# A two-layer attention and feed-forward kernel: the first layer's feed-forward and the second layer's attention rounds written as one program

## The chip, the cores and the metric

The kernel runs on one core of a Trainium2 chip. The metric is the device time of one execution in microseconds (us). A core has five engines with queues of their own that work in program order: TensorE (PE, matrix products into the PSUM banks), VectorE (DVE), ScalarE (ACT), GpSimd (POOL) and SyncE (SP, here only a queue that starts DMAs). They wait for each other through semaphores.

## The reference

Input x is 8 x 256 tokens of width 512 and a context of the same shape. Two layers follow, each an attention-like block and a feed-forward, added to x.

```
x = x + L0_xattn(layernorm(x), ctx)      # decay-masked retention, 4 heads of 128
x = x + L0_ffn(layernorm(x))             # ternary weights, rounded activations, 512 -> 1408 -> 512
x = x + L1_xattn(layernorm(x), ctx)      # mLSTM, 16 heads of 32
x = x + L1_ffn(x)                        # shared expert + 32 experts, 4 for each token
```

The change touches the second and the third line.

```
# L0_ffn
h = silu(bitlinear(x, w1)) * bitlinear(x, w3);  return bitlinear(h, w2)
# L1_xattn, q = layernorm(x), k = v = ctx
ig = concat(q, k, v) @ Wi + bi;  fg = concat(q, k, v) @ Wf + bf
F = cumsum(log_sigmoid(fg))
log_D[s, t] = F[s] - F[t] + ig[t] for t <= s, else -inf
D = exp(log_D - max_t log_D)
C = (q k^T / sqrt(32)) * D
h = C / (max(|sum C|, exp(-max)) + eps) @ v, then a norm by head
```

## The kernel before, in words

The 2048 tokens are 16 tiles of 128. `layers_kernel` (line 1647) calls `layer0_attention`, then `layer1_constants` (833) and `Gates` (449), `layer0_ffn` (571), `layer1_attention` (861) and `layer1_ffn` (1430). In `layer0_ffn` and `layer1_attention` the order of the instructions on PE, ACT and DVE (and POOL in the latter) is written by hand, inside `tc.manual_schedule`; elsewhere a planner orders them.

**The feed-forward** (lines 722 to 777) goes over the 16 tiles t. In a step PE makes the products of tile t in three chunks of 512, 512 and 384 hidden columns, eight bf16 matmuls each (`products`, line 581, matmuls at 590): four with w1 into a bank `p1`, four with w3 into a bank `p3`, two banks of each. ACT applies Silu to p1 (`silu`, 598), DVE multiplies with p3 (`gated`, 603). Then the tile's rows are rounded: DVE takes the largest value (`largest`, 607) and its scale (611 to 621), ACT scales (`shifted`, 616), DVE rounds to bf16 (`hidden_rounded`, 626), and a DMA turns the result. That rounding runs one tile behind. Two tiles behind, PE makes the output (`output`, 632, 11 matmuls into a bank `py`); three behind, DVE adds it to x (`added`, 637) and takes the statistics of the next layer norm (`stats`, 109). Inverse square roots are made on DVE by 13 small operations (`rsqrt`, 82, spread by `rooted`) for groups of 4, 2, 2, 4, 2, 1 and 1 tiles. A finished tile is normed on ACT (`norm_next`, 696), turned by four PE transposes (`turn_next`, 704) and copied by ACT to `qT` (711).

**The gates.** `Gates.context` (491) and `Gates.queries` (500) add up ig and fg of all tokens in one bank `pg`, 32 rows for each chunk of 512 tokens. `Gates.kept` (507) copies half of it to SBUF and `Gates.chain` (509) turns that half into F, the running maximum and the parts: PE sorts the rows (517), DVE adds the biases (522, 525), ACT takes Abs, Exp and Ln (528 to 532), DVE two scans (537, 542), and two rows are each split into three bf16 parts (552, 556), which DMAs write to DRAM (`parts_d`, 557). The first half (batches 0 to 3) runs through the chain at the feed-forward's end, lines 741 to 828; the second half in the rounds 0 to 14 of the attention, one step a round (line 1125). After the last tile comes a tail, lines 785 to 827: the last two outputs, the last norms and transposes, the rest of the queries and of the first chain.

**The rounds** of `layer1_attention` (`round_`, 1102) go over 32 blocks, a batch of 256 tokens by four groups of four heads, in a pipeline. In round n PE makes the exponents of block n from the parts (`decays`, 899: a bf16 matmul of 128 rows at 909 and one that adds the mask at 910, three times) and ACT applies Exp (914); PE makes the scores of block n-1 (`weights`, 929 and 933) and DVE multiplies them with the exponentials (937); PE multiplies block n-2 with the values (`heads`, 950) and block n-3 is turned back (`back`, 965). `values(b)` (881) reads a batch's values and parts from DRAM by SP's queue. `tail` spreads norms and sums of a finished batch over the following rounds on DVE, ACT and POOL (`squares` 987, `scaled` 1000, `attended` 1007 and 1008). The attention has PSUM banks and SBUF tiles of its own, and its constants (`left`, `right`, 869 to 878) are laid down by POOL and DMAs.

## Time and profile before

| | |
|---|---|
| median of 3 runs | 1096.8 us |
| all three | 1096.8, 1101.62, 1096.58 us |
| the profiled execution | 1101.73 us |
| its span, first to last instruction | 1099.9 us |
| PE / DVE / ACT / POOL busy | 1020.0 / 535.0 / 398.4 / 395.5 us |
| mean granted TensorE clock | 0.960 |

The page gives busy time by engine, the span in 40 slices (a digit is tenths of busy time; PEclk is the granted clock), and the chain that ended last. Views of the trace give the same by stretch (`from:to`, its length, then busy time and count of instructions for PE, weight load, DVE, ACT, POOL, granted clock, DMA share, GB/s) and instruction by instruction (start, duration, engine, line, operation, output<-inputs, shapes, count, and in brackets the idle time before and what ended it). In this execution the feed-forward's loop runs from 246 to 375, the tail to 403, the rounds from 403 on.

### The profile page before, as it was taken

What the parts mean: (1) busy time and instruction counts of PE and PEld (TensorE: products, weight loads), DVE (VectorE), ACT (ScalarE), POOL (GpSimd) and SP (SyncE); (2) the same over time, 40 slices, a digit from 0 to 9 for tenths busy, and PEclk for the clock granted to TensorE, in tenths of its full rate; (3) what the DMA queues carried; (4) which work ended last, traced back from release to release, by engine and by line L of the source; (5) the groups of instructions that cost most, each with busy time, mean ns of one, the idle gap of its engine ahead of it and who ended that gap; (6) DMA issues with size and microseconds to landing.
All of it is one profiled execution on the core that took longest, in us unless ns stands there. A gap on an engine that the chain in (4) does not pass through costs nothing.

```text
span 1099.9 us, 14847 instructions
## 1 busy us (share of the span) xinstructions
PE 1020.0 (93%) x5226; PEld 618.8 (56%) x5226; DVE 535.0 (49%) x1504; ACT 398.4 (36%) x680; POOL 395.5 (36%) x375
## 2 busy tenths in 40 slices
PE   7979799989999888999889899999999999999994
PEld 5746366634444345566534444555666666777782
DVE  6545555468999826888842992112221221121120
ACT  4455235136677536576631101221122222212211
POOL 0144522240000300376670223554455555545522
PEclk9989899999999868899989999999999999999997
DMA  9776321013234420212122325777777788889872
GB/s 342 275 274 216 131 93 48 1 30 59 55 70 56 117 68 27 77 61 71 39 88 81 128 84 162 177 200 189 174 199 203 203 207 235 228 226 252 239 198 35
DMA packets 101748, 154.42 MB, mean 140 GB/s; under 512 B 39812, under 2 KB 42500, under 8 KB 101640
## 3 DMA queue, kind: packets, MB, share of 16 engines
q1 hardware_dynamic: 81872, 106.68, 31.0%
q0 software_dynamic: 19552, 46.60, 19.0%
q8 instruction: 43, 0.70, 0.3%
q14 instruction: 41, 0.34, 0.1%
q10 hardware_dynamic: 240, 0.10, 0.0%
HBM read 110.42 MB, written 32.96 MB: 130 GB/s over the span
## 4 chain that ended last, share of the span: by engine, by line
PE 69%; DVE 13%; DMA 6%; POOL 4%; ACT 3%; issue 3%; SPq 0%; DVEq 0%; POOLq 0%; ACTq 0%
PE po L1478 13%; PE pg L1461 12%; PE pu L1461 12%; PE pz L380 3%; PE pw L325 3%; PE pt L1518 3%; PE p L590 3%; PE py L632 2%; DVE am L607 2%; PE pqk L929 2%; DMA vc_d<-raw 2%; PE pd L909 2%; PE num L950 2%; DMA raw<-in_ctx 1%; PE po L1168 1%
## 5 line engine op out<-in xcount | busy, mean ns | idle before, releaser
L1466 DVE TENSOR_TENSOR act<-pu,sg 128x264 f32<-128x264 f32 (+22 forms) x68 | 31.9, 469 | 314.7 <-PE pu L1461 308.5
L1503 POOL DMA_INDIRECT xg<-h_d,tok_of x85 | 83.3, 980 | 198.7 <-DVE of L1513 63.6
L1522 POOL DMA_INDIRECT out_x<-eo,to x85 | 133.0, 1564 | 54.9 <-ACT eo L1560 34.5
L1478 PE MATMUL po<-w,act 128*128 128x512 f32 (+10 forms) x456 | 143.1, 489 | 0.0
L1461 PE MATMUL pg<-xT,w 128*128 128x216 f32 (+21 forms) x512 | 136.5, 410 | 0.6 <-issue 0.6
L1461 PE MATMUL pu<-xT,w 128*128 128x216 f32 (+21 forms) x512 | 133.3, 403 | 0.0
L1560 ACT ACTIVATE eo<-po,slotw 128x512 f32<-128x512 f32 (+10 forms) x114 | 65.6, 576 | 176.9 <-PE po L1478 168.5
L1461 PEld LDWEIGHTS pg<-xT,w 128*128 128x128 f32 x512 | 93.9, 191 | 34.1 <-issue 18.7
L1461 PEld LDWEIGHTS pu<-xT,w 128*128 128x128 f32 x512 | 96.8, 190 | 26.2 <-issue 5.6
L1465 ACT ACTIVATE sg<-pg 128x264 f32<-128x264 f32 (+22 forms) x68 | 28.5, 419 | 204.5 <-PE pg L1461 192.3
L1478 PEld LDWEIGHTS po<-w,act 128*128 128x128 f32 (+10 forms) x456 | 54.1, 155 | 57.4 <-issue 47.9
L590 PE MATMUL p<-wq,xqT 128*128 128x512 bf16 (+1 forms) x384 | 80.3, 362 | 5.0 <-DVE qi L611 4.6
L937 DVE SCALAR_TENSOR_TENSOR ct<-pqk,xe 128x768 f32<-128x768 f32 x64 | 58.2, 951 | 21.7 <-PE pqk L933 16.7
L590 PEld LDWEIGHTS <-xqT 128*128 128x128 bf16 x384 | 37.2, 98 | 48.4 <-issue 10.1
L1519 DVE TENSOR_TENSOR xT<-pt,nw 128x512 f32<-128x512 f32 (+12 forms) x85 | 51.1, 601 | 21.0 <-PE pt L1518 20.8
L325 PE MATMUL pw<-wg,xnT 128*128 128x512 f32 x128 | 61.1, 622 | 0.0
L380 PE MATMUL pz<-wo,wyT 128*128 128x512 f32 x128 | 57.9, 595 | 2.1 <-ACT wyT L374 2.1
L914 ACT ACTIVATE xe<-pd 128x512 f32<-128x512 f32 x96 | 55.1, 596 | 11.0 <-PE pd L910 10.0
L1518 PEld LDWEIGHTS pt<-ident,xg 128*128 128x128 f32 (+15 forms) x340 | 39.2, 140 | 24.8 <-PE po L1478 10.5
L109 DVE BATCH_NORM_STATS2 st<-x 128x6 f32<-128x512 f32 x64 | 43.8, 685 | 15.8 <-POOL x L1008 10.2
L1518 PE MATMUL pt<-ident,xg 128*128 128x128 f32 (+15 forms) x340 | 47.2, 260 | 1.4 <-DMA xg<-h_d,tok_of 0.8
L363 POOL TENSOR_TENSOR y<-y,gam 128x512 f32<-128x512 f32 x16 | 20.9, 1304 | 76.0 <-DVE y L79 72.1
(295 smaller groups left out, 1671.1 us busy)
## 6 DMA issues: line engine op xcount, KB each, us to landing
w<-in_w SPq DMA_DIRECT2D x32, 1024.0 KB
w<-in_w SPq DMA_DIRECT2D x32, 512.0 KB
wst<-in_w1T SPq DMA_DIRECT2D x8, 704.0 KB
wst<-in_w3T SPq DMA_DIRECT2D x8, 704.0 KB
wst<-in_w2T SPq DMA_DIRECT2D x6, 768.0 KB
x<-in_x SPq DMA_DIRECT2D x16, 256.0 KB
ctxT<-in_ctxT_d SPq DMA_DIRECT2D x4, 1024.0 KB
raw<-in_ctx SPq DMA_DIRECT2D x16, 256.0 KB
```

The source lines that it names most:

```text
L325: nc.tensor.matmul(pw, lhsT=xnT[c][:, k, o : o + P], rhs=wg[:, k, :], start=k == 0, stop=k == KD - 1)
L380: nc.tensor.matmul(pz, lhsT=wyT[:, k, :], rhs=wo[:, k, :], start=k == 0, stop=k == KD - 1)
L590: nc.tensor.matmul(pp[:, : z - a], lhsT=xqT[:, k, :], rhs=w[:, k, a:z], start=k == 0, stop=k == KD - 1)
L914: nc.scalar.activation(out, pd, AF.Exp)
L937: nc.vector.scalar_tensor_tensor(ct[:, r : r + 2, :], pqk[:, :, : S + P], 1.0 / math.sqrt(HD1), xe[:, r : r + 2, :], ALU.mult, ALU.mult,)
L1461: nc.tensor.matmul(pp[:, :n], lhsT=w[:, k, cols], rhs=xT[:, k, :n], start=k == 0, stop=k == KD - 1)
L1478: nc.tensor.matmul(po[h * at : h * at + n, :cols], lhsT=act[:, m, j * P : j * P + n], rhs=w[:, m, h * cols : (h + 1) * cols], start=m == 0 ...
L1503: nc.gpsimd.indirect_dma_start(out=xg[:n], out_offset=None, in_=h_d, in_offset=bass.IndirectOffsetOnAxis(ap=g.tok_of[:n, r, j : j + 1], ax ...
L1518: nc.tensor.transpose(pt[:, k, :n], xg[:n, k * P : (k + 1) * P], g.ident[:n, :n])
L1519: nc.vector.tensor_mul(xT, pt[:, :, :n], g.nw.unsqueeze(2).to_broadcast([P, KD, n]))
L1522: return nc.gpsimd.indirect_dma_start(out=g.out, out_offset=bass.IndirectOffsetOnAxis(ap=rows, axis=0), in_=eo, in_offset=None, compute_op ...
L1560: nc.scalar.activation(eo[:n, at : at + cols], po, AF.Copy, scale=w[r][:n, j : j + 1])
```

## The change

1. `layer0_ffn` and `layer1_attention` become one function `layers_joined`, with `layer1_rounds` inside, in one hand-written schedule that also covers POOL and SP. PSUM: the pairs `pqk` (2 x 2 banks) hold p1 and p3 together, `dec` (2) the outputs and the first half's gates, `num` and `back` the transposes and `pg`. SBUF: the tiles of the feed-forward take the names of the rounds' tiles; the rounds' buffers for finished heads, their squares and a third buffer of exponentials lie in the ternary weights' place.
2. The first half's queries come at the end of tile 12, its chain in tiles 13 to 15; `values(0)` is issued before the tail. The tail is spread over rounds 0 to 4, the queries of token chunks 2 and 3 are made by `Gates.late`, and the second half's chain runs from round 5 on, four steps a round.
3. The gate logarithm is min(fg, 0) + ln(0.5 + 0.5 |tanh(fg / 2)|). The first half takes ACT's Tanh, Abs and Ln, the second half Tanh and Abs and a polynomial on DVE.
4. There are six part buffers instead of three; the first half's casts go to ACT, as does `kept`.
5. `left` and `right` are one tile each with four batches in strips of 32 rows, so a decay matmul has 32 rows instead of 128. They are set up before the feed-forward, `right` by four ACT copies in tiles 0 to 3.
6. The root groups are 4, 4, 4, 2, 2 tiles.

```diff
     def kept(self, h):
-        self.g.nc.vector.tensor_copy(self.gs[rows], self.pg[rows])
+        self.g.nc.scalar.copy(self.gs[rows], self.pg[rows])
+    def late(self, c, pg):
+        rows = slice(c * 2 * H1, (c + 1) * 2 * H1)
+        for k in range(KD):
+            self.g.nc.tensor.matmul(
+                pg[rows], lhsT=self.W[:, k, :], rhs=self.g.qT[c][:, k, :], start=k == 0, stop=k == KD - 1
+            )
+        self.g.nc.vector.tensor_add(self.gs[rows], pg[rows], self.gs[rows])
...
-        nc.scalar.activation(af, fg, AF.Abs)
-        nc.scalar.activation(af, af, AF.Exp, scale=-1.0)
-        nc.scalar.activation(af, af, AF.Ln, bias=g.ones[r, 0:1])
-        nc.vector.scalar_tensor_tensor(fg, fg, 0.0, af, ALU.min, ALU.subtract)
+        nc.scalar.activation(af, both[r, 1], AF.Tanh, bias=self.half[r, 0:1], scale=0.5)
+        nc.vector.tensor_scalar(fg, both[r, 1], self.bif[r, 1:2], 0.0, ALU.add, ALU.min)
+        yield
+        nc.vector.tensor_scalar(ig, both[r, 0], self.bif[r, 0:1], None, ALU.add)
+        if h == 0:
+            nc.scalar.activation(af, af, AF.Abs)
+            nc.scalar.activation(af, af, AF.Ln, bias=self.half[r, 1:2], scale=0.5)
+            yield
+            nc.vector.tensor_add(fg, fg, af)
+        else:
+            nc.scalar.activation(af, af, AF.Abs)
+            yield
+            nc.vector.tensor_scalar(af, af, -0.5, None, ALU.add)
+            yield
+            nc.vector.tensor_scalar(M, af, LOG[-1], None, ALU.mult)
+            for c in LOG[-2:0:-1]:
+                yield
+                nc.vector.scalar_tensor_tensor(M, M, c, af, ALU.add, ALU.mult)
+            yield
+            nc.vector.scalar_tensor_tensor(fg, M, LOG[0], fg, ALU.add, ALU.add)
...
+                (nc.vector.tensor_copy if h else nc.scalar.copy)(part, rest)
...
+    for n in range(P // 32):
+        for part in range(3):
+            nc.gpsimd.affine_select(out=g.head, ...)
+    nc.gpsimd.memset(g.left, 0.0)
+    for n in range(P // 32):
+        nc.gpsimd.memset(g.left[n * 32 : n * 32 + KR], 1.0)
+def layer1_right(g, k):
+    g.nc.scalar.copy(g.right[:, k], g.head.unsqueeze(2).to_broadcast([P, HG, S]))
...
-            p1 = ps.tile([P, 512], F32, tag="p1", name="p1")
-            p3 = ps.tile([P, 512], F32, tag="p3", name="p3")
+            both = ps.tile([P, 2, CH], F32, tag="pqk", name="p13", bufs=2)
...
+                if t == 13:
+                    times(1, first)
...
+                if t >= 14:
+                    times(3, first)
...
+                if t == 12:
+                    gates.queries((0, 1))
                     gates.kept(0)
...
+            rounds.begin()
+            hidden_scale(late)
+            turn_next("num")
+            turn_next("back")
+            added(late - 2)
+            stats(late - 2)
+            copy_next()
+            shifted(("h", late), h[late])
             copy_next()
             norm_next()
             norm_next()
+            output(late - 1)
+            rooted(late - 2, 4)
+            hidden_rounded(late)
+            rooted(late - 2)
+            added(late - 1)
+            stats(late - 1)
...
+            def between(n, place):
                 if n == 0:
+                    if place == 1:
+                        turn_next("num")
+                        turn_next("back")
+                    if place == 4:
+                        copy_next()
+                        copy_next(nc.vector)
+                        norm_next()
+                        norm_next()
+                if n == 1:
+                    if place == 2:
+                        gates.late(2, bank("num", "pgl"))
+                    if place == 3:
+                        output(late, "back", 1)
...
+                if n == 2:
...
+                    if place == 3:
+                        added(late)
+                        stats(late)
+                        rooted(late, 6)
+                    if place == 4:
+                        times(NT, first)
+                        rooted(late)
+                        norm_next()
+                        norm_next()
...
+                    if place == 3:
+                        gates.late(3, bank("dec", "pgl", 2))
+                if n >= 5:
+                    if place in (1, 4):
+                        times(2, second)
```

`between(n, place)` is called at five places of round n: 0 after the first two exponents, 1 after `back`, 2 after the third exponent, 3 after `weights`, 4 after `heads` and the batch's tail. `late` there is tile 15; `times(n, chain)` takes n steps of a chain.

## The prediction

> **What bounds the kernel now.** I read the page first, then the stage table of busy time and granted clock, then the chain of waits and the timelines of PE, ACT and DVE around the place where the first layer's feed-forward ends.
>
> ```profile
> span 1099.9 us, 14847 instructions
> ...
> PE 1020.0 (93%) x5226; PEld 618.8 (56%) x5226; DVE 535.0 (49%) x1504; ACT 398.4 (36%) x680; POOL 395.5 (36%) x375
> ...
> PE   7979799989999888999889899999999999999994
> ...
> PEclk9989899999999868899989999999999999999997
> ```
>
> PE is busy 93% and carries 69% of the chain that ended last. But slices 13 to 15 (from 357 us) show a granted clock of 8, 6, 8 tenths, and a busy PE at half clock does half the work. The stage table puts numbers on it (columns: us, busy time of PE, PEld, DVE, ACT, POOL, granted clock, DMA share, GB/s):
>
> ```profile
> 246.00:345.00 99.00, 94.00 (x475) 45.28 (x476) 92.92 (x231) 67.35 (x88) 0.00 (x0) 0.98 0.32 58
> 345.00:375.40 30.40, 30.40 (x152) 14.16 (x150) 26.51 (x62) 18.36 (x25) 5.54 (x9) 1.00 0.43 85
> 375.40:403.00 27.60, 18.56 (x74) 10.04 (x74) 14.83 (x64) 11.46 (x16) 3.02 (x4) 0.67 0.35 103
> 403.00:428.30 25.30, 21.88 (x158) 11.06 (x157) 9.18 (x13) 13.95 (x24) 0.00 (x0) 0.68 0.09 24
> 428.30:461.90 33.60, 31.41 (x342) 19.56 (x338) 28.56 (x50) 19.27 (x45) 10.49 (x7) 0.90 0.26 73
> ```
>
> Row 1 is the feed-forward's loop: DVE 92.9 of 99 us, so DVE and PE are both at their limit. Rows 3 and 4 are the join: its tail, then rounds 0 to 4 of the second layer. No engine is full and the clock is 0.67: latency bounds it. Row 5 is rounds 5 to 12: 33.6 us where eight steady rounds of 3.38 us (425.01 to 428.39 in the chain) are 27.0. Three lines say what the join waits for:
>
> ```profile
> 390.76 0.28 DVE L552 CAST part<-sw 64x256 bf16<-64x256 f32 x1 [5.83 <-DMA parts_d<-part]
> ...
> 409.15 0.49 DVE L522 TENSOR_SCALAR sw<-gates,bif 64x256 f32<-64x256 f32 x1 [6.19 <-PE gates L517]
> ...
> 416.85 0.58 PE L909 MATMUL pd<-right,left 128*128 128x512 bf16 x1 [3.32 <-ACT xe L914]
> ```
>
> DVE stands 5.83 us for a part buffer whose DMA is issued by ACT behind copies; 6.19 us for the gates of the second half; PE stands 3.32 us while ACT loads the Ln and then the Exp table.
>
> **The join, term 1.** PE work left after output(13), which ends at 373.0, at full clock: output(14) and output(15), 2 x 2.37 = 4.7; eight transposes of a tile, 8 x 0.44 = 3.5; late(2) and late(3), 8 passes of 0.22 each (16 took 3.56), 3.6; rounds 0 to 4, which are short of back (0.45), pqk (0.88) and heads (0.79) where the pipeline is not filled: 1.3 + 2.1 + 2.9 + 3.4 + 3.4 = 13.1. Sum 24.9 us. All of it can start, since the first half's parts are on their way in tile 15 and values(0) is issued before the tail.
>
> New waits: round 0's second pd takes the bank of py(14), free only after added(14). On DVE that stands behind largest(h,15) 1.6, hidden_scale 0.45, added and stats 1.5, four root steps 0.8, hq 0.85, ten root steps 1.9, added 0.7: 7.8 us after gated(15,2), which is itself 0.7 after chunk 2. PE gets there in 2.37 + 0.88 + 2.37 + 0.43 = 6.05, so it waits about 2.4. The Exp table (1.28) and three Exp hold late(2)'s copies: 1. Tiles 14 and 15 are normed only after added, stats and 14 root steps on DVE, beside two 0.95 us products a round: PE stands some 2.5 at their transposes in rounds 3 and 4. About 6 us in all. Round 5 starts at 373.0 + 24.9 + 6 = 404 against 428.3 now: **24.4 us won**. At half clock for half of it (the 0.67 of today) it would be 12 less; without the waits 6 more.
>
> **The loop, term 2.** The root chain at tile 8 goes (13 small operations of 0.17 to 0.19 with their gaps, 2.4 us; that tile took 8.66 against 7.52 beside it): 1.1 won. The first half's gates move from the tail into tiles 13 to 15. DVE gets two sums (0.97) in tile 13, 3.9 (one addition and a subtraction 0.42 each, two scans 0.69, addition, negation, two subtractions) in tile 14, 0.84 and the root chain of 2.4 in tile 15. Tile 13 has cover: 3.56 of queries, now at the end of tile 12, and 1.87 of gates matmuls. Tiles 14 and 15 have none for the excess: their DVE work without input rounding is 7.5 - 1.6 = 5.9, so 9.8 and 9.1 against PE's 7.56: 3.7 lost. ACT takes Tanh, Abs, Ln, up to three table loads of 1.28 and six casts: 1 lost at tile 13. Four copies layer1_right (128x1024; 0.8 to 1.1 us by the 0.81 of the DVE cast L852 and the 1.08 of two 512-column Exps) fit the ACT idle of 1.4 to 2.2 us before silu; without it up to 1 each.
>
> Products now take a pair of banks, so the p1 half of chunk 2 waits for gated(t,0), too:
>
> ```profile
> 333.69 0.81 PE L590 MATMUL p<-wq,xqT 128*128 128x384 bf16 x4 [1.73 <-DVE qi L611]
> ```
>
> A line of the stage table at 2 us a row, from the tile that lost the clock:
>
> ```profile
> 300.00:302.00 2.00, 2.00 (x9) 1.30 (x8) 1.97 (x5) 1.58 (x4) 0.00 (x0) 0.50 0.04 8
> ```
>
> Today four of eight matmuls (0.65) run before that wait. Where DVE sets the pace, PE regains them; priced at nothing, at most 0.65 to 0.79 a chunk. It shows the clock halved after a 1.66 us wait for the same cause that ended at 299.23, while 333.69's 1.73 did not halve it: 0 to 3 for such a drop, up or down.
>
> The Trainium skill (TensorE: Matmul & The Clock Gate, A second HAM failure mode: psum-queue depth-cycling) says that short PE stops at every bank change can make the clock swing. That speaks against the pairs. It gives no price per stop; by its half clock alone each swing would cost what the row at 300 shows, some 1.5 to 3 us.
>
> Start of the loop: the context gates wait for Wkv (PE idle 2.62 until 246.0), whose weights are fetched by POOL's queue. layer1_constants now puts 9 selects (0.20), a memset (0.95) and four of 15 rows (0.94) on POOL, 6.5 us in all. Issued behind them the fetch costs 6.5, between them 0; the 0.81 cast that leaves DVE could win as much. Today's order mixes fetches and selects, so I take 2. Term 2: -3.7 - 1 - 2 + 1.1 = **5.6 lost**, from +2 to -14.
>
> **Rounds 5 to 12, term 3.** The second half's chain moves here whole: two sums 0.98, two scalar operations 0.57, nine polynomial steps 3.8, two scans 1.38, three others 1.13, six casts 1.74, four subtractions 1.68: 11.3 us. DVE's other work in row 5 is 28.56 less the 7.4 of lines 544 to 556: 21.1. Sum 32.4, so DVE becomes the bound. Then there is POOL:
>
> ```profile
> 448.22 1.96 POOL L1000 TENSOR_TENSOR hid<-hid,rsq 128x1024 f32<-128x1024 f32 x1 [12.65 <-DVE rsq L102]
> ...
> 448.44 2.02 DVE L556 TENSOR_TENSOR sw<-sw,part 64x256 f32<-64x256 f32 x1
> ...
> 452.72 1.89 POOL L987 TENSOR_TENSOR sq<-hid 128x1024 f32<-128x1024 f32 x1
> ...
> 452.84 1.92 DVE L552 CAST part<-sw 64x256 bf16<-64x256 f32 x1
> ```
>
> A subtraction of 0.42 and a cast of 0.29 last until POOL's operation ends: 3.2 lost. At four steps a round the parts fall in rounds 9 to 11, just where POOL works 9 us on end. Three such stops give 4.8 (bounds 0 and 9). 32.4 + 4.8 = 37.2 against 33.6: **3.6 lost**, from 1 won to 9 lost. Against that the second half's two table loads leave; they are in term 1.
>
> By row, Exp after Abs costs 1.31 (370.67 to 371.98), so the load is all of a switch. The skill (ScalarE: Activation LUTs, What ACT_TABLE_LOAD costs) puts 2.66 on a switch with its drain, and (Table sets) names a set with both exp and ln; this trace loads between the two, at 370.68 and 372.41. By the page's price the first half's loads would cost 4 more in tile 13. That Exp and Tanh share a set is on the same page; no run here shows it, and if not, two loads of 1.28 return.
>
> From round 13 on nothing changes: the same rounds, buffers in the same rotation. The 32-row decay matmuls are priced as now; the pqk products already run on 32 rows.
>
> **Sum.** 24.4 - 5.6 - 3.6 = 15.2 won. The profiled execution took 1101.73 (span 1099.9 and 1.8 around it), 4.9 above the median 1096.8; it would become 1086.5, the median 1081.6. I forecast **1081**.
>
> **Rivals.**
> - **A, the forecast**, 60%: 1070 to 1091. Within the terms' middles.
> - **B, given back**, 20%: the join closes, but the half clock stays in rounds 0 to 11 and each part waits for POOL: 24.4 - 8 - 5.6 - 9 = 2 won to about 8 won with one of them alone; 1092. For it: the clock fell within 2 us at 376. Against: PE's list is unbroken but for 6 us.
> - **C, bank pairs, slower**, 9%: at every chunk the pair is still held, 0.79 lost on each of 48, 38 us; 15 - 38 gives 1119, and it turns slower from some 20 chunks on. Against: gated(t,1) ends at 358.76 and its bank is wanted at 360.0.
> - **D, cheaper**, 11%: no waits in the join, the loop's excess hidden, 24.4 + 6 - 3 = 27 won: 1069. For it: DVE idles 5 us for PE in row 5.
> - That it does not do what it says, the rounds still waiting for the parts' trip to DRAM and back, would add two transfers of 1.80 (the parts DMA at 388.94): 1085, within A.
>
> Faster by over 0.5% (below 1091.3; half a per cent is about what a measurement can tell): A 58, D 11, half of B 10: 0.79. Within: 0.12. Slower: 0.09. The range takes in A, D and most of B: 1067 to 1098.
>
> **What would show it.** Right: in the stage table the rounds begin some 25 us earlier, clock above 0.85 across the join, no 5.8 us wait for parts_d and one Ln load instead of two; DVE over 90% busy in rounds 5 to 11, with casts stretched beside POOL. Wrong: PE waits on DVE h L603 at most chunks (C), a long PE gap before L491 (start), or clock 0.5 in the rounds (B).

## The result and the profile after

The changed kernel takes 1133.8 us (median of four executions, 1129.2 to 1141.5) against 1099.2 us for the kernel before in the same comparison: 1.032 times as long, 95% interval 1.025 to 1.039. The forecast was 1081, with 1098 as its upper end, so both the sign and the size were wrong. The four executions lie 12 us apart, and the granted clock goes with them: 0.955 and 0.956 in the two short ones, 0.946 and 0.936 in the long ones. The profiled execution is the longest, 1141.5 us.

The page of the changed kernel, in the rows that answer to those shown of before:

```profile
span 1139.6 us, 14726 instructions
...
PE 1054.8 (93%) x5196; PEld 623.9 (55%) x5210; DVE 536.7 (47%) x1484; ACT 402.4 (35%) x686; POOL 392.4 (34%) x379
...
PE   6979799969999779999998898999999999999994
...
PEclk9989899989999876579998998999999999999998
```

PE was busy 1020.0 us before and is busy 1054.8 us now, with 30 matmul records fewer. Busy time times the mean clock (0.960 and 0.936) is 979 and 987, so most of the 35 us is the same work at a lower clock. The dent of PEclk that had 8, 6, 8 tenths is now deeper and longer: 8, 7, 6, 5, 7.

The stage table shows where (the columns are those of the stage table of before). The stages are the loop from its first product to the end of output(13), the join from there to round 5, rounds 5 to 12, and rounds 13 to the end of the last `back`:

```profile
242.71:389.40 146.69, 128.61 (x613) 59.55 (x624) 122.62 (x293) 93.69 (x128) 10.34 (x32) 0.94 0.30 54
389.40:443.27 53.87, 43.18 (x222) 19.51 (x223) 21.90 (x54) 20.62 (x34) 0.00 (x0) 0.71 0.11 30
443.27:501.58 58.31, 55.75 (x348) 28.58 (x347) 37.04 (x66) 22.05 (x47) 10.65 (x7) 0.56 0.08 24
501.58:587.15 85.57, 83.21 (x895) 48.51 (x892) 68.06 (x154) 60.60 (x128) 54.62 (x47) 1.00 0.23 77
```

The same four stages took 133.3, 55.3, 33.6 and 84.5 us before. So the loop lost 13.4, the join won 1.4 where 24.4 were forecast, rounds 5 to 12 lost 24.7, and the rest lost 1.1. Row 3 is the one to look at: PE is busy 55.75 of 58.31 us, it waits for almost nothing, and the clock is 0.56. A busy share of 96% at that clock is no evidence that PE does all it can.

PE's timeline of the changed kernel (start, duration, engine, line, operation, output<-inputs, count, and in brackets the idle time before and what ended it) has the waits of the loop's start and of the join, and two matmuls of a steady round:

```profile
254.19 3.64 PE L499 MATMUL pg<-ctxT,Wkv 128*32 128x512 f32 x16 [8.09 <-DVE Wkv L470]
...
404.53 5.92 PE L521 MATMUL pgl<-qT,Wif 128*32 128x512 f32 x8
...
425.78 1.25 PE L731 MATMUL back<-turn,numT 128*128 128x132 f32 x4 [5.89 <-ACT numT L724]
...
501.58 0.39 PE L675 MATMUL pd<-right,left 32*128 32x512 bf16 x1
501.89 0.28 PE L676 MATMUL pd<-lateb,identb 128*128 128x256 bf16 x1
```

ACT's timeline of the same kernel shows what stands in front of those:

```profile
253.00 1.04 ACT L628 CAST right<-head 128x1024 bf16<-128x1024 f32 x1 [5.44 <-POOL head L609]
...
379.51 0.41 ACT L576 CAST sw<-sw 64x256 bf16<-64x256 f32 x1 [4.93 <-DVE sw L578]
...
386.61 0.41 ACT L576 CAST sw<-sw 64x256 bf16<-64x256 f32 x1 [2.23 <-DVE sw L578]
...
423.95 1.52 ACT L1131 ACTIVATE xn<-x,nb,rsq 128x512 f32<-128x512 f32 x2 [4.82 <-DVE nb L1116]
425.38 0.35 ACT L724 COPY numT<-num 128x256 f32<-128x256 f32 x1
```

Five readings follow from these rows. At the start, the weights of the context gates are fetched by POOL's queue behind the constants (8.09 us), and ACT's first copy of `right` waits for the last of twelve selects on POOL (5.44). In tile 15 the first half's casts on ACT wait for subtractions on DVE (4.93, 2.23), and `silu` of the same tile stands behind them. `late(2)` takes 5.92 us for eight passes. In round 3 `back` waits 5.89 us for the copy of `numT`, which takes 0.35 but stands on ACT behind two norms that wait for the roots of tile 15. And from the start of a decay matmul of 32 rows to the start of its mask it is 0.31 us at full clock, where it was 0.23 with 128 rows (rows of before under e2); a round in which PE never waits is 3.83 us instead of 3.38.

### The profile page after: what moved, and what is told of

Its sections match the earlier page's. It is cut to its first block, busy times and chain, and to the rows that moved or that the text cites. A ratio compares the mean times of both kernels' runs of the same rounds, so it can differ in the third digit from the quotient of the medians.

```text
span 1139.6 us, 14726 instructions
## 1 busy us (share of the span) xinstructions
PE 1054.8 (93%) x5196; PEld 623.9 (55%) x5210; DVE 536.7 (47%) x1484; ACT 402.4 (35%) x686; POOL 392.4 (34%) x379
## 4 chain that ended last, share of the span: by engine, by line
PE 72%; DVE 13%; DMA 6%; POOL 3%; ACT 2%; issue 2%; SPq 0%; POOLq 0%; ACTq 0%; DVEq 0%
PE po L1561 13%; PE pg L1544 12%; PE pu L1544 12%; PE pw L329 3%; PE pz L384 3%; PE pt L1601 3%; PE pd L675 3%; PE num L716 2%; PE pqk L695 2%; PE pd L676 2%; DVE am L1045 2%; PE p L1028 2%; DVE h L1041 2%; DMA raw<-in_ctx 2%; PE back L731 2%
## 5 line engine op out<-in xcount | busy, mean ns | idle before, releaser
L1544 PE MATMUL pu<-xT,w 128*128 128x216 f32 (+21 forms) x512 | 133.3, 403 | 0.0
L1544 PEld LDWEIGHTS pu<-xT,w 128*128 128x128 f32 x512 | 96.8, 190 | 26.2 <-issue 5.6
L753 POOL TENSOR_TENSOR held<-held 128x1024 f32<-128x1024 f32 x7 | 13.3, 1902 | 201.3 <-ACT held L735 201.3
L1028 PEld LDWEIGHTS <-xqT 128*128 128x128 bf16 x384 | 37.7, 99 | 52.9 <-issue 17.3
L384 PE MATMUL pz<-wo,wyT 128*128 128x512 f32 x128 | 57.7, 594 | 1.4 <-ACT wyT L378 1.4
L1601 PEld LDWEIGHTS pt<-ident,xg 128*128 128x128 f32 (+15 forms) x340 | 39.2, 140 | 24.2 <-PE po L1561 10.5
L113 DVE BATCH_NORM_STATS2 st<-x 128x6 f32<-128x512 f32 x64 | 43.9, 686 | 16.1 <-POOL x L774 10.1
L703 DVE SCALAR_TENSOR_TENSOR ct<-pqk,xe 128x768 f32<-128x768 f32 x44 | 40.2, 952 | 19.1 <-PE pqk L699 19.1
L675 PE MATMUL pd<-right,left 32*128 32x512 bf16 x96 | 43.3, 451 | 5.6 <-DVE x L1077 3.0
```

The lines of the kernel that those rows point to most:

```text
L113: g.nc.vector.bn_stats(st, x)
L384: nc.tensor.matmul(pz, lhsT=wyT[:, k, :], rhs=wo[:, k, :], start=k == 0, stop=k == KD - 1)
L675: nc.tensor.matmul(pd, lhsT=lhsT, rhs=rhs, start=True, stop=False)
L1028: nc.tensor.matmul(both[:, m, : z - a], lhsT=xqT[:, k, :], rhs=w[:, k, a:z], start=k == 0, stop=k == KD - 1)
L1544: nc.tensor.matmul(pp[:, :n], lhsT=w[:, k, cols], rhs=xT[:, k, :n], start=k == 0, stop=k == KD - 1)
L1601: nc.tensor.transpose(pt[:, k, :n], xg[:n, k * P : (k + 1) * P], g.ident[:n, :n])
```

## The experiments

The theory after the result: (1) the decay matmuls of 32 rows cost time in each round and keep the clock down once the join has halved it; (2) the last queries, (3) the norms ahead of `numT`, (4) the casts of tile 15 and (5) the fetch behind the constants are the waits that ate the join and the loop; (6) the second half's parts meet POOL. The rivals: the clock stays down because of the join's stalls and DVE's load, not because of the rows; the bank pairs are slow; or a wait that is taken away only uncovers the next.

The table gives every run: median, ratio to the kernel before with its interval, and in the profiled execution the time from the loop's first product to output(0), from the start of output(13) to round 5, of rounds 5 to 12, of rounds 13 to 15, and of the whole stretch that the change rewrote, from the loop's first product to the end of the last `back`, in us.

| run | median | ratio | to output(0) | output(13) to round 5 | rounds 5-12 | 13-15 | rewritten stretch |
|---|---|---|---|---|---|---|---|
| before | 1099.9 | 1 | 21.3 | 57.7 | 33.6 | 10.1 | 306.7 |
| changed | 1133.8 | 1.032 (1.025-1.039) | 30.1 | 57.9 | 58.3 | 11.5 | 344.4 |
| e1 changed, 128 rows | 1114.9 | 1.013 (1.008-1.018) | 25.4 | 52.9 | 45.4 | 10.2 | 322.7 |
| e2 before, 32 rows | 1112.1 | 1.010 (1.007-1.012) | 22.9 | 58.8 | 36.7 | 14.6 | 316.0 |
| e3 changed, weights first | 1138.8 | 1.033 (1.031-1.036) | 29.4 | 53.1 | 53.6 | 11.5 | 333.2 |
| e4 before, bank pairs | 1101.8 | 1.001 (0.998-1.003) | 24.2 | 55.4 | 33.6 | 10.1 | 307.4 |
| e5 e1 + late together | 1110.3 | 1.009 (1.006-1.012) | 25.4 | 46.1 | 46.9 | 10.2 | 316.2 |
| e6 e1 + casts on DVE | 1115.2 | 1.013 (1.009-1.018) | 26.2 | 50.3 | 46.8 | 10.2 | 320.8 |
| e7 e1 + norms behind | 1111.1 | 1.011 (1.007-1.014) | 25.5 | 42.0 | 51.9 | 10.2 | 317.1 |
| e8 e1 + parts held | 1111.2 | 1.011 (1.007-1.014) | 25.5 | 52.9 | 34.6 | 19.4 | 319.3 |
| e9 five repairs | 1098.1 | 0.998 (0.995-1.000) | 21.8 | 42.3 | 40.9 | 11.9 | 305.7 |
| e10 e9 but 32 rows | 1109.0 | 1.009 (1.005-1.013) | 29.8 | 43.1 | 52.7 | 11.5 | 324.0 |
| e11 e9 with ACT's log | 1096.4 | 0.996 (0.994-0.998) | 21.8 | 40.8 | 38.8 | 11.3 | 300.4 |
| e12 e11, parts behind gated | 1093.5 | 0.995 (0.993-0.997) | 21.8 | 42.7 | 37.4 | 11.9 | 298.3 |
| e13 e10 with 64 rows | 1104.7 | 1.004 (1.002-1.006) | 23.6 | 43.3 | 43.8 | 11.5 | 308.3 |

The stretches are of one execution each: the longest of the changed kernel, the shortest of e1 and of e3. What lies outside the last column is nearly the same code in every run and took 786 to 795 us in these executions, so medians can differ by a few us for reasons outside the change. The intervals of e1, e5, e7 and e8 overlap. What e5 to e8 gained over e1 is therefore read from the stretches and is not shown by the medians.

### e1: the changed kernel with 128 rows

```diff
-        of = slice(b % HG * 32, b % HG * 32 + 32)
-        keys, rows = g.left[of, k], g.right[of, k]
+        keys, rows = left[b % 2][k], right[b % 2][k]
...
```

`left[1]` and `right[1]` are pieces of the held tiles that are free from round 1 on; POOL sets the first and copies the second by DMA in round 1, and an odd batch takes 16 small DMAs instead of 4. With one strip, POOL lays three selects instead of twelve and two memsets of `left` instead of five.

> The changed kernel with decay matmuls over 128 rows again: two pairs of left and right tiles, one a batch in turn, the second pair in the ternary weights' place and filled in round 1 (16 small DMAs for an odd batch instead of 4; three memsets and nine selects of POOL fewer at the start). Main theory: a matmul of 32 rows leaves most of the array idle and shows the weight load of the mask behind it, so that the clock, once halved in the join, doesn't rise again. Then the rounds 5 to 12 take 34 to 40 us instead of 58.3, their granted clock is above 0.8, a full-clock round falls from 3.83 to 3.4, and the time is 1100 to 1112 (of it up to 5 from the shorter constants at the start). Rival 1: the clock stays halved because the join has stalls and the second chain keeps DVE the bound; then rounds 5 to 12 take over 50 us, and the time stays within 8 of 1134, of it 5 from the constants.

Measured: 1114.9, 18.9 less by the medians (two executions of 1110.6 and two of 1119.2 and 1120.6, so the median lies between two pairs). Its stage rows for rounds 5 to 8 and 9 to 12:

```profile
428.50:445.93 17.43, 16.36 (x178) 10.14 (x177) 11.13 (x21) 10.42 (x24) 1.89 (x1) 1.00 0.09 31
445.93:473.92 27.99, 19.09 (x174) 11.81 (x171) 25.39 (x45) 9.55 (x23) 8.76 (x6) 0.82 0.11 29
```

The clock is back at 1.00 in rounds 5 to 8, where the changed kernel had 0.62, and rounds 5 to 12 take 12.9 less. The main theory holds for the clock, and e2 shows its weight load; of the time, 4.7 lie at the loop's start (30.1 to 25.4, the shorter constants), and 45.4 is more than the 34 to 40 expected. What is left of rounds 9 to 12 is DVE: busy 25.39 of 27.99 us. DVE's timeline of this run, where it splits the second half's rows in parts:

```profile
455.84 2.00 DVE L576 CAST sw<-sw 64x256 bf16<-64x256 f32 x1
457.87 1.35 DVE L578 TENSOR_TENSOR sw<-sw 64x256 f32<-64x256 f32 x1
459.26 1.15 DVE L576 CAST sw<-sw 64x256 bf16<-64x256 f32 x1
460.44 2.00 DVE L578 TENSOR_TENSOR sw<-sw 64x256 f32<-64x256 f32 x1
462.48 1.15 DVE L576 CAST sw<-sw 64x256 bf16<-64x256 f32 x1
```

A cast takes 0.29 and a subtraction 0.42 elsewhere in this profile; these five take 7.65 instead of 1.71. POOL works almost without a gap from 455.74 to 464.73, and each of the five ends within 0.3 us after one of POOL's operations. PE waits 7.35 us for the product that DVE has queued behind them.

### e2: the kernel before with 32 rows

```diff
-                keys, rows = left[b % 2][:, k], right[b % 2][:, k]
+                keys, rows = left[b % 2][:32, k], right[b % 2][:32, k]
```

> The kernel before with one change: its decay matmuls read the first 32 rows of left and right. Main theory: a full-clock round goes from 3.38 to about 3.8, and after the tail's stalls the clock stays at half through round 12 or so as in the changed kernel: 28 rounds by 0.4 is 11, and 15 to 25 more from the clock: 1110 to 1135. Rival 1 (the join's stalls and the second chain set the clock): the rounds cost 0.1 more at most, 1097 to 1101. Between: only the longer full-clock round, 1105 to 1110, clock back at full by round 5.

Measured: 1112.1, 12.2 more than the kernel before. Rounds 5 to 8 of this run:

```profile
431.99:447.31 15.32, 15.32 (x173) 8.75 (x169) 11.22 (x20) 9.94 (x22) 1.89 (x1) 1.00 0.15 43
```

Four rounds in 15.32 us are 3.83 each; before they were 13.52, 3.38 each. So one slice in one line costs the kernel before 1% of its time. Where the 0.1 us of each pair goes, the weight loads (PEld) show. Before, with 128 rows:

```profile
438.46 0.39 PE L909 MATMUL pd<-right,left 128*128 128x512 bf16 x1
438.47 0.10 PEld L910 LDWEIGHTS <-identb 128*128 128x128 bf16 x1
...
438.69 0.27 PE L910 MATMUL pd<-lateb,identb 128*128 128x256 bf16 x1
```

and in this run, with 32:

```profile
443.48 0.38 PE L909 MATMUL pd<-right,left 32*128 32x512 bf16 x1
...
443.79 0.10 PEld L910 LDWEIGHTS <-identb 128*128 128x128 bf16 x1 [0.23 <-issue]
443.80 0.28 PE L910 MATMUL pd<-lateb,identb 128*128 128x256 bf16 x1
```

The mask's weights are loaded as soon as a decay matmul of 128 rows has started, but only 0.31 us after the start of one of 32 rows, right ahead of the mask itself. The load of the next 32 rows waits in the same way, to 0.21 after the mask's start, where with 128 rows it comes at 0.00.

The clock, though, is 1.00 here: it came back after the join. So 1112.1 lies just inside the main theory's range (1110 to 1135) without the halved clock that this range rested on: the outcome lies between the two theories. The long rounds are due to the rows alone; that the clock stays halved needs more than the rows. Nor is the 12.2 made of 28 longer rounds of 0.4, as expected: in the profiled executions rounds 3 to 15 take 59.3 instead of 51.2, with the clock after round 12 in it, and rounds 16 to 30 take 62.7 instead of 62.4. That 28 by 0.4 comes near is luck. Only after the stall of round 12 does this run stay slow for longer than before (rounds 13 to 15: 14.6 against 10.1).

### e3: the gates' weights fetched first

```diff
-            layer1_constants(g, wp)
             gates = Gates(g, wp)
+            layer1_constants(g, wp)
```

> The changed kernel with the gates' weights fetched ahead of the second layer's constants on POOL's queue (two lines exchanged). Main theory: the wait of 8.09 us ahead of the context gates falls to 2.6 or less, 5.5 won at the start of the loop: 1126 to 1130. Rival: the wait is only moved (the loop is bound by DVE and catches up), within 2 of 1134.

Measured: 1138.8, no gain. The rival was right that the wait is only moved, for a reason that it didn't name, and 1138.8 is not within its 2 of 1134. PE's wait for the gates falls from 8.09 to 0.53, but the constants now stand behind the fetch, and ACT's first copy of `right` waits for them:

```profile
252.97 1.04 ACT L628 CAST right<-head 128x1024 bf16<-128x1024 f32 x1 [6.89 <-POOL head L609]
```

It starts 11.8 us after the loop's first product, later even than the 10.3 of the changed kernel. `silu` of the second chunk is behind it on ACT, `gated` behind that, and PE waits 6.81 us there. Constants and fetch stand in one list on POOL, and either order leaves one of them late. In e9, with the short list of 128 rows and the fetch first, the first output comes 21.8 us after the first product, as before.

### e4: the kernel before with bank pairs

```diff
-            p1 = ps.tile([P, 512], F32, tag="p1", name="p1")
-            p3 = ps.tile([P, 512], F32, tag="p3", name="p3")
+            both = ps.tile([P, 2, 512], F32, tag="p13", name="p13")
+            p1, p3 = both[:, 0], both[:, 1]
...
```

> The kernel before with p1 and p3 of a chunk in one pair of banks, as the changed kernel has them, and nothing else. Main theory: the pairs cost little, 0 to 4 us in the loop of 129 us (from the first product to the end of output(13) 133.3): 1097 to 1102. Rival C of the prediction (every chunk waits for gated two chunks back): 10 us or more, the loop at 143 or longer.

Measured: 1101.8, ratio 1.001 (0.998 to 1.003). The whole difference of the loop, 2.9 us, lies before the first output; from there to output(13) both take 109.6. Rival C of the prediction falls, and so does the fear that the pairs make the clock swing: it is 0.99 over the loop in both.

### e5: the last queries together (on e1)

```diff
-                        gates.late(2, bank("num", "pgl"))
...
-                        gates.late(3, bank("dec", "pgl", 2))
+                        gates.late(bank("dec", "pgl", 2))
```

`late` then goes over both chunks for each k, so that neighbouring matmuls write different strips of 32 partitions.

> The changed kernel with 128 rows (the run of that name is the base of this and the next three), and with the queries of token chunks 2 and 3 made together in round 4, one k after the other for both chunks, instead of chunk 2 in round 1 and chunk 3 in round 4. Main theory: a strip of 32 columns alone takes as long as two strips side by side; in the base the two take 6.15 us (clock 0.5 to 0.7) and 3.9, mixed with heads; together 3.6 at full clock. Then rounds 0 to 5 shrink by 4 to 7 and the time falls by as much, to 1108 to 1111 against the base's 1115. Rival: PE has time there since it waits for ACT and DVE (numT, ct) anyway; then the wait ahead of back in round 3 grows, and the time stays within 2.

Measured: 1110.3, 4.6 less than e1 by the medians; in the profiled executions 6.8 is won by round 5 and 1.5 given back in rounds 5 to 12. In e1 a stretch of five matmuls of `late(3)` takes 2.33 us at full clock; in this run a stretch of ten, for two chunks, takes 2.34 (first row of e1, second of e5):

```profile
424.29 2.33 PE L521 MATMUL pgl<-qT,Wif 128*32 128x512 f32 x5
...
418.50 2.34 PE L522 MATMUL pgl<-qT,Wif 128*32 128x512 f32 x10
```

The second strip cost nothing beside the first.

### e6: the first half's casts on DVE (on e1)

```diff
-                (nc.vector.tensor_copy if h else nc.scalar.copy)(part, rest)
+                nc.vector.tensor_copy(part, rest)
...
-                (nc.sync if n or h else nc.scalar).dma_start(...)
+                nc.sync.dma_start(...)
```

> The base (changed kernel with 128 rows) with the first half's six casts on DVE instead of ACT, and its parts written by SP's queue. Main theory: in tiles 14 and 15 ACT and DVE wait for each other at every part (2.2 and 4.9 us ahead of casts), and silu of tile 15 stands behind these; tile 15 takes 12.2 us instead of 7.2. With the casts on DVE (6 x 0.29 = 1.74 more there) output(13) ends 3 to 5 us earlier: 1110 to 1112. Rival: DVE is the bound of tiles 14 and 15, then 1.7 more, 1115 to 1118.

Measured: 1115.2 against 1114.9, nothing. ACT's waits for subtractions are gone, and PE still waits 3.13 us in tile 15 (3.46 in e1): the first `gated` of the tile stands on DVE behind the same parts. The main theory named the wrong queue. The rival, that DVE is the bound there, fits better: e12 puts the parts behind that `gated`, wins 3.1 at output(13) and gives 2.8 of it back at output(14).

### e7: the last norms behind the copy (on e1)

```diff
-                        norm_next()
-                        norm_next()
+                if n == 3 and place == 2:
+                    norm_next()
+                    norm_next()
```

> The base (changed kernel with 128 rows) with the last two norms made in round 3 instead of round 2 (behind the copy of numT instead of ahead of it), their transposes and the last queries one round later, so that the second half's chain starts a few steps later. Main theory: PE's wait of 6.1 us ahead of back in round 3 falls to 1 to 2, and 3 to 5 us are won by round 5: 1110 to 1112. Rival: the root chain on DVE sets that time wherever the norms stand; the wait moves to the transposes of round 4, within 2 of the base.

Measured: 1111.1, 3.8 less by the medians and 5.6 in the rewritten stretch. From round 3 to round 4 it is 4.5 us instead of 12.3. Round 5 is reached 10.9 us earlier, but the last queries and the second half's chain now start in round 5, and rounds 5 to 12 take 6.5 more. Both theories hold in part: the wait was the order on ACT, and some 60% of what it gave came back as the next.

### e8: the second half's parts held back (on e1)

```diff
-                if n >= 5:
+                if 5 <= n < 9 or n >= 12:
                     if place in (1, 4):
                         times(2, second)
+                if n == 9 and place == 1:
+                    times(3, second)
```

> The base (changed kernel with 128 rows) with the second half's parts held until rounds 12 and 13: steps 1 to 19 in rounds 5 to 9 as before, the six parts, the transposes and em in rounds 12 and 13. Main theory: five operations on parts that took 7.65 us (1.71 alone) stood in POOL's stretch of 9 us, and PE waited 7.4 us for the product behind them. Without that the rounds 5 to 12 fall from 45.4 to 38 to 40, and the time by 5 to 7: 1108 to 1110. Rival: POOL's stretch holds DVE's other operations as well (or the parts meet POOL's next stretch in round 13), within 3 of the base.

Measured: 1111.2, 3.7 less by the medians and 3.4 in the rewritten stretch, short of the 5 to 7. Stage rows of rounds 9 to 12 and 13 to 15:

```profile
446.72:463.93 17.21, 15.34 (x173) 9.80 (x169) 14.82 (x32) 9.29 (x22) 6.92 (x5) 1.00 0.11 33
463.93:483.28 19.35, 14.69 (x132) 8.97 (x129) 14.74 (x37) 7.54 (x18) 7.99 (x8) 0.74 0.15 41
```

Rounds 9 to 12 fall from 27.99 to 17.21, so the parts beside POOL were worth 10.8 us. Rounds 13 to 15 rise from 10.2 to 19.4: there the parts meet a root chain on DVE, PE waits 2.48 and 2.18 us for DVE's products, and the clock falls to 0.74.

### e9, e10, e11: the repairs together

e9 joins five: 128 rows, weights first, queries together in round 4, the sum and roots of tile 15 put on DVE's queue in round 1 with the norms behind `numT`, and the second chain at seven steps a round, so that its parts come before POOL's stretch.

```diff
-                    if place in (1, 4):
-                        times(2, second)
+                    if place in (1, 3, 4):
+                        times(1 if place == 3 else 3, second)
```

> The changed kernel with five repairs together: decays over 128 rows; gates' weights fetched first; the last queries of both chunks together in round 4; the sum, statistics and roots of tile 15 put on DVE's queue in round 1 (ahead of the transposes of round 2) and the last norms behind the copy of numT; and the second half's chain at seven steps a round instead of four, so that its parts are split before POOL's stretch in rounds 9 to 11. Main theory: the losses measured one by one add up: base 1115, less 3 (weights), 6 (queries), 4 (norms), 6 to 8 (parts): 1094 to 1099, level with the kernel before or a little under it. Rival: the terms overlap (a wait that goes uncovers the next; the chain at seven steps a round makes DVE the bound of rounds 6 to 8), 1101 to 1106.

Measured: 1098.1, ratio 0.998 (0.995 to 1.000). The terms add up nearly in full: 16.8 less than e1 (17.0 in the rewritten stretch), where 19 to 21 were expected of them one by one. The rounds still lose: DVE's parts now hold PE in round 8 (a wait of 3.58), and rounds 5 to 12 take 40.9 against 33.6 before. e10 is the same with decays over 32 rows.

> The run before with decay matmuls over 32 rows as in the changed kernel. Main theory: 28 rounds of 0.45 cost 12 as they did in the kernel before, and the clock that the remaining stalls of the join halve comes back later: 12 to 20 more than the run before, 1107 to 1118. If the clock stays at half through round 12 again: 1120 or more. Rival (the rows matter only because the join has long stalls): at most 8 more.

Measured: 1109.0, 10.8 more. Its ten executions fall into two groups, six of 1104.0 to 1109.1 with a clock of 0.967 to 0.973 and four of 1118.1 to 1125.0 with 0.952 to 0.956. The profiled one is of the second group. Its rounds 9 to 12:

```profile
452.32:479.01 26.69, 26.69 (x169) 13.37 (x169) 12.42 (x27) 10.69 (x23) 8.42 (x6) 0.51 0.09 26
```

and the same rounds of e9:

```profile
442.20:457.30 15.10, 15.10 (x169) 9.32 (x169) 10.43 (x24) 9.79 (x23) 7.35 (x6) 0.88 0.16 46
```

Both stretches follow a stall of PE of some 3.5 us, and in both PE is busy for the whole stretch. With 128 rows the clock is back after one round (4.96 us); with 32 rows it is at 0.51 for 26.69 us, and returns in round 13. That the longer group is the clock that doesn't come back fits the mean clocks, but no execution of the shorter group was profiled. Not all of the 10.8 is the rows' own: this run has the long list of constants again, and its first output comes 8.0 later.

e11 is e9 with ACT's logarithm in place of the polynomial (`if h >= 0:` for `if h == 0:`), four steps a round.

> The run with all five repairs, with ACT's logarithm for the second half too instead of the polynomial (ten steps of DVE fewer, 3.9 us; two more table loads of 1.28 us on ACT in front of Exp) and four steps a round, so that the parts fall in rounds 7 to 9. Main theory: two loads hold the Exp of a round for 2.6 us while DVE has room, so this is 0 to 3 us slower than the polynomial. Rival: DVE is the bound of rounds 6 to 8, and without the polynomial 2 to 4 us are won.

Measured: 1096.4, ratio 0.996 (0.994 to 0.998). That is 1.8 less than e9, but the intervals overlap, so no difference between the two logarithms is shown; nor are they all that differs, since e9's chain takes seven steps a round. The rewritten stretch is 5.3 shorter in the one execution of each, of it 2.0 in rounds 5 to 12.

### e12: the parts behind the gate's products

```diff
+                if last:
+                    times(2, first)
                 products(t, 1)
...
-                    times(3, first)
+                    times(3 if t == 14 else 2, first)
                 products(t, 2)
```

with two more at the end of tile 15 instead of three at the end of tile 14, and the casts and DMAs of e6.

> The run with all repairs and ACT's logarithm, with the first half's six casts on DVE, its parts written by SP's queue, and the parts two at a time behind each of tile 15's three products with the gate (gated) instead of three ahead of the first and three behind the second. Main theory: tile 15 takes 12.2 us instead of 7.2 since its first gated stands behind the parts, the rounding's scale and the sum on DVE; behind it the parts cost their own 1.7 and 1.7 us on a DVE that is full: tile 15 falls to 9 or 10, and the time by 2 to 3, to 1093 to 1095. Rival: the parts arrive later in DRAM, and round 0, which reads them, waits for that: within 1 of 1096.4.

Measured: 1093.5, ratio 0.995 (0.993 to 0.997): the shortest of all runs, below both kernels (against e11 the intervals overlap). From output(12) to output(13) it is 9.06 us instead of 12.2, as expected; output(14) then follows 7.99 later instead of 5.2, so within the loop most of it comes back. Its join and its rounds 5 to 12:

```profile
375.32:415.64 40.32, 29.86 (x223) 15.85 (x223) 25.09 (x69) 21.39 (x36) 3.35 (x8) 0.92 0.28 78
415.64:453.06 37.42, 31.92 (x349) 19.77 (x347) 25.79 (x53) 23.26 (x50) 9.28 (x7) 0.95 0.13 38
```

The clock is 0.92 and 0.95 where the changed kernel had 0.71 and 0.56. Rounds 5 to 12 take 37.4, close to the 37.2 that the prediction's term 3 gave them, but without the polynomial that stands in its sum, so this is no confirmation.

### e13: 64 rows

```diff
-        of = slice(b % HG * 32, b % HG * 32 + 32)
+        of = slice(b % 2 * 64, b % 2 * 64 + 64)
```

> The run with all repairs but the rows (decays over 32 rows, four batches in strips of 32) with strips of 64 rows for two batches in turn. Theory one, the share of the array's rows that work decides whether the clock comes back: a full-clock round of about 3.8 or a little less, and the clock of rounds 9 to 12 between 0.51 (32 rows) and 0.88 (128 rows), the time 1100 to 1107. Theory two, any matmul that doesn't use all rows shows the weight load behind it: 3.83 a round and the clock as with 32 rows, 1107 to 1112. Theory three, only the 32-row strip is slow: as with 128 rows, 1097 to 1100.

Measured: 1104.7 (1.004, 1.002 to 1.006), ten executions within 6 us, with no second group. Rounds 9 to 12:

```profile
445.09:463.30 18.21, 18.21 (x170) 10.11 (x171) 11.39 (x26) 10.11 (x23) 8.45 (x6) 0.82 0.14 39
```

A full-clock round is 3.83 us (463.3 to 467.1 and on), the same as with 32 rows, and the gap from a decay matmul to its mask is 0.32: for the price of a round it doesn't matter whether 64 or 96 rows are missing (theory two). The clock, 0.82, lies between that of 32 rows in e10 and of 128 in e9 (theory one): after the same stall it is back in 6.7 us, where e9 took 4.0 and e10 26.8. But e10's row is of its longer group, and one profile of each can't tell 64 rows from e10's shorter group. So the price of a round and the clock are two effects; that the clock goes by the share of rows is not shown.

## Why the prediction was wrong, point by point

- **What bounds the kernel**: right. The join is latency at a low clock, the loop DVE and PE.
- **"The 32-row decay matmuls are priced as now; from round 13 on nothing changes"**: the step that failed first. The evidence offered was that the pqk products already run on 32 rows, but these follow each other, while a decay matmul alternates with a mask of 128 rows, whose weights are loaded late behind it (e2). It costs 0.45 in a PE-bound round (3.83 instead of 3.38), and after a stall the clock stayed at half in the changed kernel (0.56) and in e10 (0.51). By e1 the rows are worth some 14 of the 35 us lost, with the constants' 4.7 taken off (17 of 38 in the rewritten stretch). Rounds 13 on lost only 1.1, since ACT, DVE and POOL bound most of them.
- **Term 1, 24.4 won**: measured 1.4. "late(2) and late(3), 8 passes of 0.22 each": that price came from 16 matmuls of two chunks side by side; alone a pass is 0.47 at full clock and 0.74 here (6.8 us by round 5 in e5). "New waits, about 6": round 0 was foreseen (2.4, measured 3.04) and so was Exp (1, measured 1.34). The wait that mattered was not among them: the norms stand ahead of `numT` on ACT, and PE waits 5.89 for the copy, not for their transposes (e7). The clock across the join was to be above 0.85 and was 0.71. With the repairs the join is 40.3 in e12, 15.0 won.
- **Term 2, 5.6 lost**: measured 13.4. The start was to cost 2 and costs 8.8; the prediction saw the fetch on POOL's queue but not that ACT's copy of `right` waits for the last select of the same list (e3). Tiles 13 to 15 were to lose 4.7 and lost 3.8 (28.3 to 32.1 from output(10) to output(13)): right. The root chain was to win 1.1, and output(0) to output(10) is 80.5 instead of 81.3; since e2, with the loop of before, has 80.8, the sign is right and the size not shown. The pairs at nothing: right (e4). Output(13) itself ran 1.6 longer at a low clock.
- **Term 3, 3.6 lost**: measured 24.7. The mechanism, parts stretched beside POOL, was right and its price too small: "three such stops, 4.8" were five, and 10.8 us in rounds 9 to 12 (e8), since PE waits for the product queued behind the last of them. The rest is the rows and the clock. The polynomial, which the prediction blamed for DVE's 32.4, makes no difference that these runs can show (e11). That Exp and Tanh need no load between them, which no run had shown, the changed kernel shows: Tanh at 446.76 stands between two Exp, and after the load at 394.60 ACT loads no table until 591.57.
- **The rivals**: B said that the half clock stays in the rounds and that parts wait for POOL, which is what happened, but it left a gain of 2 to 8 us and sought the cause in the join alone. Two of the signs of being wrong that the prediction named came: the long PE gap at the start (8.09) and a clock of 0.5 in the rounds. C was put on the pairs; e4 clears them. The slower rival should have been the clock on rows.

What stays open is why the clock stays at half with 32 rows in some executions and returns in others, and why it returns at round 13 in both the changed kernel and e10. The share of working rows is the reading that fits e1, e10 and e13 together; e2, where the clock came back with 32 rows, shows that it isn't the only condition. The traces add one fact: from 340 to 520 us of the fifteen profiles, the clock read every 0.25 us, the half clock always lasts 3.4 us or a whole multiple of it, as if it were decided anew every 3.4 us. With 128 rows it holds at most five times running (17.0 us, in the join of before), with 32 rows up to fifteen (51.0, the changed kernel); in e10 it holds ten times, and PE had no idle time in the last seven.

The Trainium skill (TensorE: Matmul & The Clock Gate, What's actually happening) says that the clock is restored after about 3.4 us of sustained work. In the kernel before, after the stall that ended at 416.85, the clock was back at 422.5, after some 6 us of work, which is the order of that figure. The row of e10, 26.69 us of unbroken work at 0.51, does not agree, and the measurement decides.

The skill (same page, Part 3, The mechanism) says in its list of what overlaps that a weight load overlaps running matmuls only if it goes to other rows of the array. The mask uses all rows, so by that rule its load would be late behind every decay matmul. Here it starts within 0.01 us of one of 128 rows and 0.31 after one of 32 or 64: the runs show something else. Ahead of that list the section also lets a load go ahead into a background weight buffer, which fits the 128 rows and doesn't tell why 32 or 64 differ.

## What to carry to other kernels

Price a matmul's shape by its neighbours: a matmul of fewer rows between matmuls of all rows (0.1 us at a change of rows here), or a strip of 32 columns without a second strip beside it, costs what its own duration doesn't show. After a stall, look at the granted clock beside the busy share, for a PE that is 96% busy at a clock of 0.56, as in rounds 5 to 12, looks full and isn't. And when work is laid into another program's queue, list for each engine what stands behind every instruction that can wait; here one list on POOL and two norms on ACT cost 8.8 and 5.9 us.

## What the hardware showed that wasn't expected

- The clock stayed at 0.50 to 0.51 for 26.7 us (e10) and from 450 to 500 us (changed kernel, PE busy 48.5 of 50).
- The half clock lasts 3.4 us or a whole multiple: all 55 such stretches between 340 and 520 us of the fifteen profiles are within 0.25 us, the step of the reading, of one, from 3.4 to 51.0.
- From a decay matmul to its mask it is 0.22 us with 128 rows, 0.31 to 0.32 with 32 or 64 (e1, changed kernel, e13). The mask's weight load starts 0.00 after the first and 0.31 after the others (medians of 57 pairs from round 13 on).
- Ten matmuls into two strips of 32 partitions take as long as five into one: 2.34 and 2.33 us (e5, e1).
- A cast of 0.29 us lasted up to 2.00 beside a POOL operation, while DVE's products that read PSUM kept their 0.95.
